# A preactivation convolution stack on one Trainium2 core: casts of tap pieces in GpSimd's row, W loads held during image loads, and another order of the opening

## The chip, the cores and the metric

The kernel runs on one core of one Trainium2 chip. The time is the device time of one execution in microseconds; the figure for a kernel is the median of its runs, and one further execution is recorded by the profiler. The engines are named as the profile names them: PE (TensorE), DVE (VectorE), ACT (ScalarE), POOL (GpSimd) and SP (SyncE, which here issues DMAs and nothing else).

## The reference

Four images of 32 x 32 pixels with 16 channels go through four residual layers. Layers 0 to 2 are of this form (G has other 3x3 taps for every output pixel; M and W join every pixel with every other):

```python
y = group_norm(x)                                        # 8 groups, eps 1e-5
first = jnp.einsum('ijpq,bpqc->bijc', M2, y)
shifted = conv3x3(y, G)            # for every output pixel ij its own 3x3 taps over the whole image
diff = relu(y[:, :, :, None, None, :] - shifted)         # b p q ij c
second = jnp.einsum('ijpq,bpqijc->bijc', W2, diff)
x = x + first - second
```

In layer 3 the group norm is convolved with the impulse response of a recursive filter, which comes from a division of two DFTs, and `x` is added. All is float32; some operands are split into two float32r pieces, `hi` (a cast) and `lo` (what is left), which are multiplied one beside the other.

## The kernel before

**The work of a layer.** A layer has 128 blocks (`NBLK`). A block is 8 output pixels of 16 channels each, so 128 rows of PSUM, with all 1024 pixels of one image in the free dimension. One call of `iteration` does one block for one image. TensorE multiplies the block's taps with the image in a PSUM pair (`pt`, four buffers); VectorE then takes `min(pt, 0) * W` and sums it in one `scalar_tensor_tensor` (L658). The centre pixel is subtracted from the taps beforehand (`minus_mid`, L475), so `pt` is already `shifted - y`.

Images 0 to 2 go through `direct`: two passes with eight of the taps (`f`, L609) and one with the ninth, in float32r pieces (`g`, also L609). Image 3 goes through `shared`, which forms what two neighbouring columns share once (L625), copies it to SBUF with ScalarE (`both_sb`, L629), does the rest (L637) and adds the two with VectorE (L645). The PSUM buffer that L625 wrote comes free with the copy L629.

**Passes.** The first 12 blocks of a layer run for images 0 and 1 and then once more for images 2 and 3; blocks 12 to 115 run for all four; the last 12 run again for (0, 1) and then (2, 3). These five stretches are called sub-passes here; they have 24, 24, 416, 24 and 24 iterations. So the next layer's images 0 and 1 can be normalised, stored and loaded while images 2 and 3 are still being finished, and the other way round.

**Taps.** Four blocks (`GC`) share one chunk of taps; each time a pass comes to a chunk is a "use" `u`, and `begin[u]` is the iteration at which it starts. `four_taps(u)` loads `f` (512 KB, by SP from F) and subtracts the centre on GpSimd (L475). `other_taps(q, at)` makes the pieces of chunk `q`: SP loads `raw` (288 KB from E); GpSimd subtracts the centre (L475) and adds rows (L508 twice); ScalarE casts `hi` (L512); GpSimd subtracts to get `lo` (L514) and issues eight DMAs (L519) that store both in DRAM, in one of eight buffers `gd`. `piece_loads(u)` has SP load `g` from `gd` (L535; 2 DMAs for images 0 and 1 alone, 12 where image 3 takes part). The tiles: `f` three buffers, `g` two, `raw`, `hi` and `lo` one each.

**W.** A W tile is 1 MB (`load_w`, L573, by SP), covers two blocks and has six buffers. `w_loads` issues tile k 24 iterations ahead of its first use (10 for tile 5 and those before it), or later, when a buffer is free.

**Images.** `make_image` runs when a pair of images has finished a layer: `group_norm`; `store_image` (`center` on VectorE, L321, the kinds of shifts and pieces by ScalarE, GpSimd and VectorE, L353 to L372, then three stores to DRAM `img`, L375 to L377); `load_image`, which issues the loads of `f<-img` and `n<-img` (L413) in turn on SP and GpSimd, and for images 2 and 3 on ScalarE too; and `copy_out` (ScalarE, L332), which the next layer's `first_term` reads.

**The order.** The schedule is written by hand, so each engine runs its instructions in the order in which the program issues them. The generators above hang in two lists: `step()`, at the end of each iteration, advances each of them to its next `yield`, and `until(at)` holds one back to iteration `at`. What a generator issues in one step therefore stands in each engine's row ahead of the next iteration's instructions. `other_taps` has its times in the pair `at`, reckoned from `need[q]`, the iteration by which the `g` loads come. Where a DMA's destination or its semaphore isn't free, the queue that issues it stands. The DMAs of SP and ScalarE take turns in eight semaphores: one more is issued only when the one eight places ahead of it has landed.

**The opening.** `first_images` makes images 0 and 1 of layer 0 from host-arranged copies (`first_f`: eight taps and `nine`) without the way through DRAM, and the `g` of uses 0 and 1 from `first_g` (`g9`, cast by ScalarE at L226, `lo` rows by VectorE at L229). Between its group norm's steps TensorE does 16 matmuls of the coefficients' DFT (`coefs`) for layer 3. `rest()` then makes images 2 and 3 by way of DRAM during the first sub-pass.

Of the kernel before, what the change touches and what calls it, by code (L numbers as in the profile page):

```python
# [36 lines left out]
def conv_stack_kernel(ctx, tc, x, M, W, first_w, first_f, first_g, F, E, h0, coef, cst, dft, idp, idq, out):  # L37
# [10 lines left out]
    ge = ctx.enter_context(tc.tile_pool(name="ge", bufs=1))  # L48
    junkp = ctx.enter_context(tc.tile_pool(name="junk", bufs=1))
# [23 lines left out]
    for t in (*yp, *ye):  # L73
# [31 lines left out]
    now = {"at": 0}  # L105
# [86 lines left out]
    def first_images(nine, g9):  # L192
# [21 lines left out]
        def last_tap(b):  # L214
            v, v8 = nine[:, b], ims_of(b)[1].rearrange("p l m -> p (l m)")
# [7 lines left out]

        def first_taps(u):
            part = g9[:, bass.ts(u, GC * P)]
            nc.scalar.copy(gn0[u], part)  # L226
            for r in (32, 96):
                lo = gn0[u][r : r + 32]
                nc.vector.tensor_tensor(lo, part[r : r + 32], lo.bitcast(F32), ALU.subtract)  # L229
            gt[u] = [gn0[u]]  # L230
# [30 lines left out]
        minus_mid(fours[0][:, 1].rearrange("r (n f) -> r n f", f=C), mid, nc.vector)  # L261
# [4 lines left out]
        for _ in range(2):  # L266
            next(norm)
        dft(0, 1)
# [8 lines left out]
        normalise(0, 0, nc.vector)  # L277
        clear(0, 0)
        normalise(0, 1, nc.scalar)
        clear(0, 1)  # L280
# [3 lines left out]
        last_tap(0)  # L284
        for k in range(2):
            normalise(1, k, nc.vector)
            clear(1, k)
# [54 lines left out]
    def store_image(a, xt, neg, rstd):  # L342
# [27 lines left out]
        for b, v in enumerate(kinds):  # L370
            to = kinds_of(ye[a], a, b)
            nc.gpsimd.tensor_copy(to[96:, :, 1:], v[96:, :, :3])  # L372
            nc.scalar.copy(to[:32, :, :3], v[:32, :, 1:])
        rows = img[a]
# [124 lines left out]
    def other_taps(q, at):  # L499
# [3 lines left out]
        raw = ge.tile([96, 3, 2 * P], F32, tag="raw", name="raw")  # L503
# [5 lines left out]
        yield from until(at[1] + 1)  # L509
# [727 lines left out]
```

## Time and profile before

| | us |
|---|---|
| three runs | 3047.81, 3042.73, 3047.37 (median 3047.37) |
| profiled execution | 3047.96, its span 3046.2, mean granted clock 0.991 |
| opening, to the first block | 0 to 16.35 |
| layer 0: sub-passes end | 80.4, 127.0, 919.9, 965.0, 1026.6 |
| layer 1: sub-passes end | 1072.3, 1118.5, 1904.3, 1949.3, 2012.2 |
| layer 2: sub-passes end | 2057.9, 2104.1, 2889.9, 2934.9, 2984.7 |
| layer 3 | 2984.7 to 3046.2 |

The ends are those of VectorE's last L658 in the sub-pass. The profiled execution lies 0.6 us over the median; sums are made against it. In the steady stretch an iteration of `direct` takes 1.93 us and one of `shared` about 1.69 on TensorE, where TensorE sets the pace; a block of images (2, 3) takes 3.75 us, and there VectorE does (three instructions of 1.22 to 1.23 us, with the small ones between). Rows of the profile name line, engine and operation, destination and source, shape and count, then busy time and mean duration, then the engine's idle time ahead of these instructions and what ended most of it. In lists of waits the three figures are the sum, the number and the mean. In timelines a row starts with its time and duration in us, and what the engine waited for stands in brackets.

### The profile page before, as it was taken

How to read it: one execution, taken by the hardware profiler on the slowest of the kernel's cores; microseconds unless marked ns; L12 is line 12 of the kernel's file. 1: busy time of each engine (PE TensorE's matmuls, PEld its weight loads, DVE VectorE, ACT ScalarE, POOL GpSimd, SP SyncE). 2: the span in 40 equal slices, each digit the busy share in tenths (PEclk: the TensorE clock that was granted, in tenths of full speed). 3: DMA queues.
4: the chain of work that ended last, by engine and by line, in shares of the span. 5: the costliest groups of instructions: out<-in, count | busy, mean ns of one | idle time of the engine just before them, and what ended most of it. 6: DMA issues, size and time to landing. Idle time of an engine off the chain costs nothing.

```text
span 3046.2 us, 53601 instructions
## 1 busy us (share of the span) xinstructions
PE 2982.4 (98%) x20884; PEld 2192.1 (72%) x20884; DVE 2412.9 (79%) x3639; ACT 307.5 (10%) x555; POOL 1070.6 (35%) x1517
## 2 busy tenths in 40 slices
PE   7999999999999899999999999989999999999998
PEld 4765666788887576678888888757567888888874
DVE  5878888888887787788888888769788888888873
ACT  1110110000001011000000100101000000000000
POOL 5435663232332433432323233343333233332300
PEclk8999999999999999999999999999999999999998
DMA  8887676656675898766666676589777776857634
GB/s 233 230 207 185 158 189 167 178 154 169 162 164 146 209 224 200 182 155 168 165 158 173 150 180 150 157 198 235 197 179 178 167 185 163 199 151 180 151 107 80
DMA packets 235589, 531.82 MB, mean 175 GB/s; under 512 B 83672, under 2 KB 93496, under 8 KB 209992
## 3 DMA queue, kind: packets, MB, share of 16 engines
q1 hardware_dynamic: 162832, 472.72, 61.3%
q0 software_dynamic: 66480, 47.05, 6.7%
q10 hardware_dynamic: 6024, 8.63, 1.4%
q8 instruction: 165, 2.70, 0.4%
q14 instruction: 88, 0.72, 0.1%
HBM read 481.67 MB, written 45.92 MB: 173 GB/s over the span
## 4 chain that ended last, share of the span: by engine, by line
PE 84%; DVE 3%; DMA 2%; issue 1%; SPq 0%; ACT 0%; POOL 0%; DVEq 0%; POOLq 0%; ACTq 0%
PE pt L609 65%; PE pt L637 14%; PE pt L625 3%; DVE junk L658 2%; PE pt L952 1%; DVE pt L645 1%; DMA f<-img 1%; DMA t<-hd 1%; PE pt L445 0%; DMA g<-gd 0%; SPq L535 0%; DMA raw<-in_E_dram 0%; SPq L413 0%; DVE st L150 0%; POOL raw L508 0%
## 5 line engine op out<-in xcount | busy, mean ns | idle before, releaser
L609 PE MATMUL pt<-f,f 64*128 64x512 f32 x9216 | 2239.4, 592 | 10.3 <-DVE junk L658 4.0
L658 DVE SCALAR_TENSOR_TENSOR junk<-pt,w 128x1024 f32<-128x1024 f32 x1536 | 1880.8, 1224 | 372.7 <-PE pt L609 256.1
L609 PEld LDWEIGHTS pt<-f,f 64*128 64x128 f32 x9216 | 1149.1, 187 | 503.6 <-issue 264.6
L609 PE MATMUL pt<-n,g 64*128 64x480 f32 x2304 | 997.0, 779 | 6.3 <-DMA g<-gd 6.2
L645 DVE TENSOR_TENSOR pt<-pt,both_sb 128x1024 f32<-128x1024 f32 x384 | 473.1, 1232 | 195.2 <-PE pt L637 164.4
L637 PE MATMUL pt<-f,f 64*128 64x256 f32 x3072 | 509.8, 378 | 3.5 <-DVE junk L658 1.2
L637 PE MATMUL pt<-n,g 64*128 64x256 f32 x3072 | 503.4, 372 | 0.0
L629 ACT COPY both_sb<-pt 128x512 f32<-128x512 f32 x384 | 224.9, 586 | 2350.5 <-PE pt L625 2265.3
L609 PEld LDWEIGHTS pt<-n,g 64*128 64x128 f32 x2304 | 314.9, 188 | 188.5 <-issue 102.9
L475 POOL TENSOR_TENSOR raw<-raw,cs 96x256 f32<-96x256 f32 x96 | 69.8, 727 | 908.6 <-DMA raw<-in_E_dram 908.3
L637 PEld LDWEIGHTS pt<-n,g 64*128 64x128 f32 x3072 | 370.2, 188 | 6.3
L514 POOL TENSOR_TENSOR lo<-raw,hi 96x512 fp32r<-96x512 f32 x96 | 121.9, 1270 | 529.3 <-ACT hi L512 529.3
L637 PEld LDWEIGHTS pt<-f,f 64*128 64x128 f32 x3072 | 293.6, 186 | 4.8 <-PE pt L625 2.6
L625 PEld LDWEIGHTS pt<-n,g 64*128 64x128 f32 x2304 | 230.8, 186 | 83.1 <-issue 35.9
L625 PE MATMUL pt<-n,g 64*128 64x256 f32 x2304 | 230.3, 279 | 20.2 <-ACT both_sb L629 20.2
L519 POOL DMA_DIRECT2D gd<-lo x384 | 226.8, 597 | 12.8 <-DMA f<-img 8.1
L519 POOL DMA_DIRECT2D gd<-hi x384 | 229.6, 603 | 3.2 <-issue 3.2
L475 POOL TENSOR_TENSOR f<-f,cs 128x512 f32<-128x512 f32 x113 | 145.6, 1289 | 192.3 <-DMA f<-in_F_dram 167.5
L508 POOL TENSOR_TENSOR raw<-raw 96x256 f32<-96x256 f32 x192 | 139.5, 727 | 15.1
L658 DVE DVE_READ_ACCUMULATOR junk<-pt,w 128x1 f32 x1536 | 127.8, 83 | 0.0
L512 ACT CAST hi<-raw 96x512 fp32r<-96x512 f32 x96 | 59.3, 618 | 189.2 <-POOL raw L508 189.0
L461 POOL DMA_DIRECT2D fd<-ft x48 | 25.2, 533 | 44.2 <-ACT ft L453 27.2
(131 smaller groups left out, 341.2 us busy)
## 6 DMA issues: line engine op xcount, KB each, us to landing
w<-in_W_dram SPq DMA_DIRECT2D x188, 1024.0 KB, 12.1
g<-gd SPq DMA_DIRECT2D x1184, 128.0 KB, 4.3
f<-in_F_dram SPq DMA_DIRECT2D x114, 512.0 KB, 3.6
raw<-in_E_dram SPq DMA_DIRECT2D x96, 288.0 KB, 9.3
gd<-hi POOLq DMA_DIRECT2D x384, 48.0 KB, 4.2
gd<-lo POOLq DMA_DIRECT2D x384, 48.0 KB, 4.5
mt<-in_M_dram SPq DMA_DIRECT2D x12, 512.0 KB, 12.7
w<-in_M_dram SPq DMA_DIRECT2D x12, 512.0 KB, 8.0
```

The costliest lines, as they stand in the source:

```text
L475: engine.tensor_tensor(v, v, m.unsqueeze(1).to_broadcast([v.shape[0], v.shape[1], C]), ALU.subtract)
L508: nc.gpsimd.tensor_tensor(raw[:, 0], raw[:, 0], raw[:, k], ALU.add)
L512: nc.scalar.copy(hi, both)
L514: nc.gpsimd.tensor_tensor(lo, both, hi.bitcast(F32), ALU.subtract)
L519: nc.gpsimd.dma_start(out=to[slot, :, k, :, bass.ts(u, 2 * P)], in_=t[48 * u : 48 * u + 48, slot].bitcast(F32),)
L609: nc.tensor.matmul(pt[:, half, px], lhsT=w[rows, at], rhs=rhs, start=k == 0, stop=k == 2)
L625: nc.tensor.matmul(both[:, half], lhsT=w[rows, at], rhs=ni[rows, dy : dy + 4, 2], start=dy == 0, stop=dy == 2)
L629: nc.scalar.copy(sb, both)
L637: nc.tensor.matmul(pt[:, half].rearrange("p (r k m) -> p k r m", k=2, m=16)[:, k], lhsT=w[rows, at], rhs=rhs, start=k == j == 0, stop=k == ...
L645: nc.vector.tensor_tensor(v, v, sb.rearrange("p h (r m) -> p (h r) m", m=16).unsqueeze(2).to_broadcast([P, 32, 2, 16]), ALU.add,)
L658: nc.vector.scalar_tensor_tensor(junk, pt.rearrange("p h m -> p (h m)"), 0.0, wts[blk // 2][:, blk % 2, :], ALU.min, ALU.mult, accum_out=a ...
L952: nc.tensor.matmul(rows.rearrange("n (j r) -> n j r", j=C)[:, :, 8 * cc :], lhsT=y(cc).rearrange("p q b -> p (q b)"), rhs=ts[k][q][:, :, : ...
```

## The change

- **The cast of the tap pieces.** `hi` is made by GpSimd instead of ScalarE (`nc.gpsimd.tensor_copy`), and `lo` is written in place over `raw`, whose pool has two buffers now. The cast, `lo` and the eight stores follow the additions in the same step; before, they came one and two iterations later. The times `at` are worked out anew: the load of `raw` 34 iterations ahead of the need at most, the rest 15 ahead.
- **W.** `now["image"]` counts images that are being stored and loaded (from `store_image` to the end of `load_image`); `w_loads` issues nothing while it isn't zero.
- **Image loads.** `load_image` issues one image per step, with a `yield` behind each; `copy_out` comes ahead of the loads in `make_image`.
- **The opening.** `g9` and `nine` take tiles of the pool `work` instead of their own; `g9`'s first part is ScalarE's first DMA but x; F of use 0 is loaded ahead of the images, the second part of `coefs` behind image 0 instead of ahead of F, F of use 1 behind image 1 instead of at iteration 2. `minus_mid` of use 0 goes from VectorE to GpSimd. The `lo` rows of `first_taps` become calls of their own (`first_lo`), one of them after `last_tap(0)`. In `rest()` images 0 and 1 are centred and copied out ahead of the store of 2 and 3. `minus_mid` of use 1 comes at iteration 3.
- **Names.** The pair of first images is called `FIRST` (0, 1, as before); the constant 24 of layer 3 is called `AHEAD`; `yq` of layer 3 lies in `ys`.

```diff
+FIRST = (0, 1)
...
+    er = ctx.enter_context(tc.tile_pool(name="er", bufs=2))
...
-    passes = [
-        (blks, batches)
-        for layer in range(3)
-        for blks, batches in (
-            (range(layer * NBLK, layer * NBLK + END), (0, 1)),
-            (range(layer * NBLK, layer * NBLK + END), (2, 3)),
-            (range(layer * NBLK + END, (layer + 1) * NBLK - END), (0, 1, 2, 3)),
-            (range((layer + 1) * NBLK - END, (layer + 1) * NBLK), (0, 1)),
-            (range((layer + 1) * NBLK - END, (layer + 1) * NBLK), (2, 3)),
-        )
-    ]
+    spans = (0, END), (END, NBLK - END), (NBLK - END, NBLK)
+    start = [[range(layer * NBLK + lo, layer * NBLK + hi) for lo, hi in spans] for layer in range(3)]
+    passes = []
+    for layer in range(3):
+        firsts = [FIRST, tuple(b for b in range(B) if b not in FIRST)] if layer == 0 else [(0, 1), (2, 3)]
+        blks = start[layer]
+        passes += [(blks[0], pair) for pair in firsts] + [(blks[1], (0, 1, 2, 3))]
+        passes += [(blks[2], pair) for pair in ((0, 1), (2, 3))]
...
-    now = {"at": 0}
+    now = {"at": 0, "image": 0}
...
+        def first_lo(u, r):
+            part = g9[u]
+            lo = gn0[u][r : r + 32]
+            nc.vector.tensor_tensor(lo, part[r : r + 32], lo.bitcast(F32), ALU.subtract)
+
         def first_taps(u):
-            part = g9[:, bass.ts(u, GC * P)]
-            nc.scalar.copy(gn0[u], part)
-            for r in (32, 96):
-                lo = gn0[u][r : r + 32]
-                nc.vector.tensor_tensor(lo, part[r : r + 32], lo.bitcast(F32), ALU.subtract)
+            nc.scalar.copy(gn0[u], g9[u])
...
-        minus_mid(fours[0][:, 1].rearrange("r (n f) -> r n f", f=C), mid, nc.vector)
+        minus_mid(fours[0][:, 1].rearrange("r (n f) -> r n f", f=C), mid)
...
         first_taps(0)
         for _ in range(2):
             next(norm)
+        first_lo(0, 32)
         dft(0, 1)
...
         last_tap(0)
+        first_lo(0, 96)
...
             first_taps(1)
+            first_lo(1, 32)
+            first_lo(1, 96)
             yield
-            pair = lambda a: (xs[:, 2 * a : 2 * a + 2], *(t[:, 2 * a : 2 * a + 2] for t in (neg, rstd)))
-            yield from store_image(1, *pair(1))
-            yield
-            load_image(0, 1)
-            copy_out(1)
-            yield
-            center(0, *pair(0))
-            yield
-            copy_out(0)
+            for a in range(2):
+                pair = slice(2 * a, 2 * a + 2)
+                at = xs[:, pair], neg[:, pair], rstd[:, pair]
+                later = [b for b in range(2) if 2 * a + b not in FIRST]
+                if later:
+                    yield from store_image(a, *at)
+                    yield
+                    yield from load_image(0, a, later)
+                else:
+                    center(a, *at)
+                    yield
+                copy_out(a)
             nc.vector.tensor_copy(avg_r, avg)
 
         todo.append(rest())
...
         yield from store_image(a, xt, neg, rstd)
+        copy_out(a)
         yield
-        load_image(layer + 1, a)
-        copy_out(a)
...
+        now["image"] += 1
...
-    def load_image(layer, a):
-
-        moves = []
+    def load_image(layer, a, batches=(0, 1)):
+
         of = lambda t: t.rearrange("p l k m -> p l (k m)")
-        for b in range(2):
+        for b in batches:
+            moves = []
...
-        queues = (nc.sync, nc.gpsimd, nc.scalar)[: 2 + a]
-        for n, (to, src) in enumerate(moves):
-            queues[n % len(queues)].dma_start(out=to, in_=src)
+            queues = (nc.sync, nc.gpsimd, nc.scalar)[: 2 + a]
+            for n, (to, src) in enumerate(moves):
+                queues[n % len(queues)].dma_start(out=to, in_=src)
+            yield
+        now["image"] -= 1
...
-        if u == 1:
-            at = 2
-        yield from until(at)
-        load_f(u)
-        yield from until(min(max(at + 8, begin[u] - 16), begin[u] - 2))
+        if u > 1:
+            yield from until(at)
+            load_f(u)
+        yield from until(min(max(at + 8, begin[u] - 16), begin[u] - 2) if u > 1 else 3)
...
-        raw = ge.tile([96, 3, 2 * P], F32, tag="raw", name="raw")
+        raw = er.tile([96, 3, 2 * P], F32, tag="raw", name="raw")
...
         for k in (1, 2):
             nc.gpsimd.tensor_tensor(raw[:, 0], raw[:, 0], raw[:, k], ALU.add)
-        yield from until(at[1] + 1)
         both = raw[:, 0::2]
-        hi, lo = (ge.tile([96, 2, 2 * P], F32R, tag=tag, name=tag) for tag in ("hi", "lo"))
-        nc.scalar.copy(hi, both)
-        yield from until(at[1] + 2)
+        hi, lo = ge.tile([96, 2, 2 * P], F32R, tag="hi", name="hi"), both.bitcast(F32R)
+        nc.gpsimd.tensor_copy(hi, both)
         nc.gpsimd.tensor_tensor(lo, both, hi.bitcast(F32), ALU.subtract)
         to = gd[q % len(gd)]
...
-    at = 0, 1
+    done = [0, 0]
     for q in sorted(need, key=need.get):
+        first = max(need[q] - 34, done[-2])
+        at = first, max(first + 3, need[q] - 15, done[-1])
+        done.append(at[1] + 1)
         tasks.append((at[0], other_taps(q, at)))
-        following = [k for k in sorted(need, key=need.get) if need[k] > need[q]][:1]
-        for k in following:
-            first = max(need[k] - 26, at[1] + 3)
-            at = first, max(first + 4, min(first + 7, need[k] - 9))
...
-            while not w_free():
+            while not w_free() or now["image"]:
...
+        g9 = [work.tile([P, GC * P], F32, tag=tag, name="g9") for tag in ("ft", "xr")]
+        nc.scalar.dma_start(out=g9[0], in_=first_g[:, : GC * P])
...
-        image_tiles(0, 0)
-        image_tiles(0, 1)
-        nine = st.tile([P, 2, 4 * PX], F32, name="nine")
-        g9 = st.tile([P, 2 * GC * P], F32, name="g9")
+        for b in FIRST:
+            image_tiles(0, b)
+        nine = [work.tile([P, 4 * PX], F32, tag=tag, name="nine") for tag in ("yt", "xo")]
         first_part = 4 * P + 2 * NCH
         coefs = st.tile([P, coef.shape[1]], F32, name="coefs")
-        for part in (slice(0, first_part), slice(first_part, coef.shape[1])):
-            nc.sync.dma_start(out=coefs[:, part], in_=coef[:, part])
+        nc.sync.dma_start(out=coefs[:, :first_part], in_=coef[:, :first_part])
+        load_f(0)
         ab = coefs[:, : 2 * P]
         ones = coefs[:, 4 * P : first_part].rearrange("p (ch r) -> p ch r", r=2)
...
-        load_f(0)
         load_first(0)
+        nc.sync.dma_start(out=coefs[:, first_part:], in_=coef[:, first_part:])
         list(load_w(2))
         load_first(1)
-        nc.sync.dma_start(out=g9[:, GC * P :], in_=first_g[:, GC * P :])
+        load_f(1)
+        nc.sync.dma_start(out=g9[1], in_=first_g[:, GC * P :])
         first_images(nine, g9)
...
-            yq = work.tile([P, 16 * (31 + S - FIRST)], F32, name="yq")
+            yq = ys[:, : 16 * (31 + S - AHEAD)]
```

More of the change, by code (lines that the diff above doesn't have):

```diff
@@ L212, in clear, with last_tap @@
                 nc.gpsimd.tensor_tensor(edge, edge, mask.to_broadcast([P, S]), ALU.mult)
-        def last_tap(b):
-            v, v8 = nine[:, b], ims_of(b)[1].rearrange("p l m -> p (l m)")
+        def last_tap(k):
+            b = FIRST[k]
+            v, v8 = nine[k], ims_of(b)[1].rearrange("p l m -> p (l m)")
             m = neg[:, B + b : B + b + 1]
@@ L276, in first_images @@
             neg, rstd = end.value
[L277 to L280, printed above, removed]
+        normalise(FIRST[0], 0, nc.vector)
+        clear(FIRST[0], 0)
+        normalise(FIRST[0], 1, nc.scalar)
+        clear(FIRST[0], 1)
         for ch in range(1, SOON):
@@ L284, in first_images @@
         last_tap(0)
+        first_lo(0, 96)
         for k in range(2):
-            normalise(1, k, nc.vector)
-            clear(1, k)
+            normalise(FIRST[1], k, nc.vector)
+            clear(FIRST[1], k)
         last_tap(1)
@@ L313, in make_image @@
         yield from store_image(a, xt, neg, rstd)
+        copy_out(a)
         yield
-        load_image(layer + 1, a)
-        copy_out(a)
+        yield from load_image(layer + 1, a)
     def center(a, xt, neg, rstd):
@@ L880, in conv_stack_kernel, with load_first @@
         soon = [st.tile([P, 2, 2, 2 * P], F32, name=f"soon{ch}") for ch in range(SOON)]
-        nc.scalar.dma_start(out=g9[:, : GC * P], in_=first_g[:, : GC * P])
-        def load_first(b):
+        def load_first(k):
             size = 8 * PX
-            for to, at in ((ims[0, b][0].rearrange("p l k m -> p (l k m)"), 0), (nine[:, b], 8 * PX)):
-                nc.sync.dma_start(out=to, in_=first_f[:, b, at : at + size])
+            to = ims[0, FIRST[k]][0].rearrange("p l k m -> p (l k m)"), nine[k]
+            for to, at in zip(to, (0, 8 * PX)):
+                nc.sync.dma_start(out=to, in_=first_f[:, k, at : at + size])
                 size = 4 * PX
-        load_f(0)
         load_first(0)
+        nc.sync.dma_start(out=coefs[:, first_part:], in_=coef[:, first_part:])
         list(load_w(2))
         load_first(1)
-        nc.sync.dma_start(out=g9[:, GC * P :], in_=first_g[:, GC * P :])
+        load_f(1)
+        nc.sync.dma_start(out=g9[1], in_=first_g[:, GC * P :])
         first_images(nine, g9)
@@ L908, in conv_stack_kernel @@
     after = (7, 6, 5, 4, 3)
-    FIRST = 24
+    AHEAD = 24
     late, ts = {}, {}
@@ L931, in of_pair @@
         return [
-            (("pair", a), 2 * i + half, y(31 - TQ * k - q - i + 16 * half - FIRST), k, q + i)
+            (("pair", a), 2 * i + half, y(31 - TQ * k - q - i + 16 * half - AHEAD), k, q + i)
             for i in range(2)
@@ L999, in norm3 @@
         for y in (
-            late["yp"][:, a, :, 31 - FIRST :],
+            late["yp"][:, a, :, 31 - AHEAD :],
             late["y3"][:, :, 31:, 2 * a : 2 * a + 2],
@@ L1162 @@
     around = np.zeros((2, S + 2, S + 2, C), x.dtype)
-    around[:, 1 : S + 1, 1 : S + 1] = x[:2]
+    around[:, 1 : S + 1, 1 : S + 1] = x[list(FIRST)]
     taps = lambda tap, half: (
```

## The prediction

> **What bounds the kernel now.** I read the page first, then TensorE's waits, a table by stage, the chain of waits through the worst stage, and last the timeline of the opening.
>
> ```profile
> PE 2982.4 (98%) x20884; PEld 2192.1 (72%) x20884; DVE 2412.9 (79%) x3639; ACT 307.5 (10%) x555; POOL 1070.6 (35%) x1517
> ...
> PEclk8999999999999999999999999999999999999998
> ```
>
> TensorE is the bound, and the change takes no matmul away. What can be won lies in TensorE's waits, in the clock that is halved around them, and in stretches where VectorE is the slower one. TensorE's longest waits:
>
> ```profile
> PE pt L625 <- ACT both_sb L629: 20.2, 2, 10.3
> PE pt L952 <- DMA t<-hd: 8.6, 2, 5.3
> PE pt L609 <- DMA g<-gd: 6.2, 1, 6.2
> ```
>
> Two waits of 10 us lead, on a ScalarE that is 10% busy. They lie in the last sub-pass (images 2 and 3) of layers 0 and 1. The table by stage sets these beside the same sub-pass of layer 2:
>
> ```profile
> 965.00:1026.60 61.60, 49.03 (x396) 36.26 (x394) 47.20 (x81) 10.62 (x23) 29.32 (x46) 0.92 0.88 213
> 1949.30:2012.20 62.90, 49.96 (x399) 36.59 (x396) 47.23 (x82) 10.61 (x23) 29.32 (x46) 0.89 0.89 213
> 2934.90:2984.70 49.80, 46.16 (x414) 34.00 (x411) 47.13 (x81) 7.12 (x13) 1.27 (x1) 1.00 0.38 100
> ```
>
> After the span come busy times of PE, PEld, DVE, ACT, POOL, then clock and DMA. VectorE does 47.1 to 47.2 us in each, so the sub-pass is VectorE's at about 50 us; the first two hold 12 and 13 us more. The chain says why:
>
> ```profile
> 993.38 12.96 DMA f<-img
> ...
> 1009.54 3.48 DMA raw<-in_E_dram
> ...
> 1013.09 0.73 POOL raw L475
> ...
> 1015.96 0.58 ACT both_sb L629
> ```
>
> And ScalarE's timeline, the row ahead of that copy:
>
> ```profile
> 1015.44 0.62 ACT L512 CAST hi<-raw 96x512 fp32r<-96x512 f32 x1 [15.27 <-POOL raw L508]
> ```
>
> SP stands in image loads that share the rings with 1 MB of W (issued 991.90). `raw` is therefore issued at 1009.54, GpSimd's three passes over it (L475, L508 twice, 0.73 us each) end at 1015.4, and the cast of it stands in ScalarE's row ahead of the copy L629 that TensorE needs. Nobody needs the cast so early; the row order alone makes it everyone's wait.
>
> **Part 1, the cast moves from ScalarE to GpSimd, with two raw buffers.** ScalarE loses 96 casts of 618 ns, GpSimd gains 96; `lo` is now written into `raw`. A GpSimd cast of 96x512 is in no row. Below it is the copy 32x480 (584 ns), above it `lo` with two inputs (1270 ns):
>
> ```profile
> L514 POOL TENSOR_TENSOR lo<-raw,hi 96x512 fp32r<-96x512 f32 x96 | 121.9, 1270 | 529.3 <-ACT hi L512 529.3
> ...
> L372 POOL COPY ye<-ys 32x480 f32<-32x480 f32 x7 | 4.0, 584 | 7.6 <-DVE ys L368 7.4
> ```
>
> I take 0.6 us, the nearer in kind. 96 x 0.6 = 58 us on an engine that is 35% busy costs nothing in the middle, where taps lead their use by some 15 iterations (29 us). The gain: in block pair (125, 2/3) VectorE's ends stand 14.72 us apart instead of the 3.75 of its neighbours, 10.97 lost; in layer 1 it is 15.09, and 0.89 at the next, 12.2 lost. A third cast delays `both_sb` at 132.75 (TensorE gap 1.49). Sum: 24.7. It goes if nothing else is late there. Next in line: the taps `g` of block 128. In the new order SP issues two W loads after the image, then F, then this `g`. I put its issue at 1003 to 1005; the W load at 974.50 landed 7.7 us after issue, nearly alone; two of them, F and `g` give 1015 to 1017.5. TensorE, 11 us earlier than now, wants it at 1018.4. It just fits.
>
> The Trainium skill speaks against this move: "GPSIMD Engine Reference", section "Key points", says that GpSimd shares its SBUF interfaces with VectorE and contends with VectorE instructions that have two SBUF inputs, and that elementwise work runs about twice as fast on VectorE. The trace agrees for two SBUF inputs: the two subtracts of L229 took 0.68 and 0.69 us with GpSimd quiet, and 1.33 us for the one at 26.89, beside `lo` on GpSimd. But VectorE's main instruction L658 reads PSUM and SBUF: 1223 ns for the 206 that lie mostly beside GpSimd's adds, 1225 for the 1177 beside none. By the rule a cast would hold VectorE for 0.6 us; some 12 casts fall into VectorE-bound sub-passes, 7 us, and the gain would be 17. By the rows it is nothing; I take the rows.
>
> **Part 2, W waits while an image is in DRAM; each image is loaded in two steps, copied out before.** The 12.96 us that `f<-img` took beside W should fall towards the 3 to 5 us of loads without it. That is off TensorE's path once the cast is gone. The price is W late: W tile 1 of the next layer moves from 991.90 to about 1002, landing near 1010 to 1012, for block 130 at about 1026. Queued behind SP's image loads are those W's, F and `g` above. Covered, by 3 us for `g` and over 10 for W; without the cover each us of lateness is a us lost, and more with the clock.
>
> **Part 3, the opening.** Now TensorE starts blocks at 16.35, and sub-pass 0 of 24 iterations at 1.933 ends at 80.4. Rows that carry it:
>
> ```profile
> 7.50 0.69 DVE L475 TENSOR_TENSOR f<-f,cs 128x512 f32<-128x512 f32 x1 [2.63 <-DMA f<-in_F_dram]
> ...
> 10.61 1.39 DVE L229 TENSOR_TENSOR g<-g,g 32x512 fp32r<-32x512 f32 x2 [1.79 <-ACT g L226]
> ...
> 35.74 1.26 POOL L475 TENSOR_TENSOR f<-f,cs 128x512 f32<-128x512 f32 x1
> ```
>
> The L475 wait leaves VectorE for GpSimd (2 us off the norm), and L229 is split and later. Then the 16 DFT matmuls (0.215 us each, from 20 in 4.30) bind: their coefficients are now loaded after F, f and nine, by bytes near 10.1, so blocks start near 13.6. Iteration 1 ends near 18.0 instead of 22.2: 4 us won, one from the clock. Next, `f` of use 1 leaves its place behind the image store: the gap of 2.42 us at 34.63 goes, and with it a half clock from 37.4 to 40.8, 1.7 us. "TensorE: Matmul & The Clock Gate", section "Why this matters for your kernels", warns of idle gaps over about 3 us; here 2.42 us already had the half clock behind it (0.50 in that stretch). By the rule this edit is worth 2.4, by the trace 4.1. I take the trace.
>
> At nothing I enter `FIRST` (the passes come out the same), `yq` in `ys` (last read by layer 1's store), and images 0 and 1's `center` and `copy_out` ahead of the image store: two L321 in 0.60 us and one L332 at 0.41 in VectorE's and ScalarE's rows, which wait for TensorE there; without that slack, 1 us on the store.
>
> So iteration 16 is reached near 45 instead of 53.5. It needs `f` and `g` of use 2, and here the new order has a price. GpSimd: `raw` for chunk 2 lands near 24.5; add-up, cast, lo 4.4 us; eight stores at 0.6, to 33.9; the same again for chunk 0, to 43.0; image store 3.1; then `f`, ready at 47.5. SP: the fourth `raw` reuses the buffer of chunk 0, which now holds `lo`, so it waits until those stores have landed, near 44.8; behind it in SP's row stand W tile 4, the image stores, F and `g`. `g` also waits for a free DMA semaphore, that of W tile 4: issued 45.3, plus 7.7. `g` issues near 53, behind image stores and F in the rings, and lands near 58.5, against 61.5 now. Then the image loads, 12 us as at 1043 to 1055, W tile 5 near 67, held by the image, landing 75 to 77, and the last six `g` of use 3 behind its semaphore, near 82 to 84, where the first shared block would want them at 78 to 80. Its VectorE end is 85.4 now, 84.5 to 88.5 then. So the 8 us won early are taken back by two `g` waits: I enter a loss of 1 us, from -8 (a gain) to +4.
>
> **Sum.** The profiled execution took 3047.96 (span 3046.2), 0.6 over the median 3047.37 of the runs. 3047.96 - 24.7 + 1 = 3024.3; I say 3024.
>
> **Rivals.** *The opening keeps its gain*: if W tile 4 and the stores land some us sooner, `g` is there near TensorE and 5 to 12 us remain: about 3015. For it: TensorE really is 8 us earlier; against: the queue above. *Transitions half won*: `g` of block 128 comes 3 to 6 us late behind two W's, with the clock 4 to 7 each time: 3024 + 11 = 3035. For it: W's median is 12.1 us to landing, not 7.7. This is also the case in which the change does not do what it says: the stall changes its name. *Slower*: the held W's are the mechanism. If two W's after the image take 14 us each in series (slow tenth of the W loads with a recorded landing), `g` of block 128 lands at 1003 + 28 + 4 = 1035 against 1018: 17 us and 2 of clock in each of two transitions, 38 - 24 = 14 slower, 3061. It decides from 12 us of stall per transition on. Against it: the rings are read in order and few others load then.
>
> **How the numbers follow.** Likeliest case 0.50 (own range 3018 to 3030), kept opening 0.25, half won 0.18, slower 0.03, transitions that lose nearly all they win 0.04 (no change). Range: 3011 to 3036, which leaves out the tails of the second and third case and the last two. Within 0.2% (6 us, about what this measurement can tell from no change): 0.04; faster 0.93, slower 0.03.
>
> **What would show it.** In the trace after: no L629 wait over 2 us; the two sub-passes at 50 to 52 us; no cast on ScalarE; a GpSimd cast of 0.5 to 0.8 us; blocks starting near 13.6; no gap near iteration 8; a `g` wait at iteration 16 of 8 to 12 us, and a short one at the first shared block. Wrong if: `g` of block 128 stops TensorE near 1017; the cast takes over 1 us; sub-pass 0 ends before 75.

## The result, and the profile after

The changed kernel takes 3048.95 us (median of 20 runs, 3043.66 to 3051.64), the kernel before 3045.56 (20 runs, 3040.87 to 3049.29). The ratio is 1.001, with a 95% interval of 1.0003 to 1.0017: slower by about a tenth of a per cent, less than the 0.2% that the prediction set as "no change". Forecast were 3024 and a chance of 0.93 for faster. The profiled execution took 3049.85 us (span 3047.7), 1.9 more than that of before.

The page's first row and clock row hardly differ from before:

```profile
PE 2982.8 (98%) x20884; PEld 2222.2 (73%) x20884; DVE 2413.2 (79%) x3638; ACT 256.4 (8%) x459; POOL 1128.7 (37%) x1617
...
PEclk8999999999999999999999999999999999999999
```

TensorE's waits in the changed kernel (sum, number, longest; the third figure of such a row is the longest single wait, also in the rows further up, where it was called the mean):

```profile
PE pt L616 <- DMA g<-gd: 17.3, 2, 10.6
PE pt L616 <- DVE junk L665: 11.4, 6, 7.4
PE pt L960 <- DMA t<-hd: 8.3, 2, 6.2
PE pt L616 <- DMA gd<-hi: 7.4, 1, 7.4
```

(L616 is the former L609, L665 the former L658, L636 the former L629.) The 20.2 us for `both_sb` are gone, as forecast. In their place stand waits for `g` and for VectorE. (In the fourth row, at 1023.21, the matmul that waits is the one that reads `g`; the releaser named is a store of pieces of another chunk, and the experiments below show which DMA it was.) The table by stage places them; first the transition from layer 0 to layer 1:

```profile
974.20:1024.80 50.60, 46.36 (x390) 34.95 (x387) 47.09 (x81) 9.61 (x21) 29.42 (x47) 1.00 0.87 214
1024.80:1079.80 55.00, 49.19 (x246) 38.53 (x246) 33.04 (x68) 2.77 (x9) 21.99 (x35) 0.91 0.85 202
```

Columns as before: stretch, span, PE, PEld, DVE, ACT, POOL, clock, DMA share, GB/s. The sub-pass (2, 3) lost its 11 us and runs at VectorE's pace; the sub-pass after it, which took 45.7 us before, takes 55.0, at a clock of 0.91. The same ledger for all kernels of this study, from the ends of VectorE's last L665 in each sub-pass of the profiled execution (us):

| kernel | layer 0: sub-pass 0 ends | sub-pass 1 | 2 | 4 | layer 1: 0 | 4 | layer 2: 0 | layer 3 |
|---|---|---|---|---|---|---|---|---|
| before | 80.4 | 46.6 | 792.9 | 61.6 | 45.7 | 62.9 | 45.7 | 61.5 |
| changed | 89.6 | 48.1 | 791.5 | 50.6 | 55.1 | 50.7 | 54.9 | 58.5 |
| 1 before, cast alone | 78.2 | 48.6 | 791.4 | 50.6 | 54.0 | 51.1 | 52.9 | 58.8 |
| 2 before, g first alone | 78.9 | 48.3 | 792.2 | 62.0 | 45.7 | 62.0 | 45.7 | 57.5 |
| 3 before, both | 81.0 | 46.6 | 791.3 | 50.6 | 49.8 | 51.0 | 50.6 | 60.4 |
| 4 changed, cast on ScalarE | 82.8 | 51.1 | 797.3 | 56.9 | 45.7 | 57.8 | 45.7 | 61.2 |
| 5 changed, no hold | 87.5 | 50.0 | 791.5 | 50.6 | 55.5 | 50.7 | 52.6 | 60.7 |
| 6 changed, g first | 84.1 | 51.3 | 791.5 | 50.6 | 50.1 | 50.7 | 49.4 | 58.3 |
| 7 changed, g first, no hold | 87.1 | 50.5 | 791.5 | 50.6 | 47.7 | 50.7 | 48.8 | 59.3 |
| 8 changed, tap times | 67.6 | 52.8 | 791.5 | 50.6 | 55.3 | 50.7 | 55.3 | 58.6 |
| 9 ... and W tile 5 early | 63.5 | 55.6 | 791.5 | 50.6 | 54.6 | 50.7 | 55.3 | 60.8 |
| 10 ... and g first, no hold | 64.7 | 54.7 | 791.5 | 50.6 | 50.4 | 50.7 | 47.3 | 61.3 |
| 11 ... and f ahead of taps | 63.0 | 50.4 | 791.5 | 50.6 | 47.8 | 50.7 | 51.1 | 59.2 |

Sub-pass 3 (45.0), those not listed of layers 1 and 2 and the last (49.8) are the same everywhere within 0.3 us. Layer 3 differs by up to 4 us between kernels with the same instructions there (57.5 to 61.5 in row "before" and rows 1 to 3), so its 3.0 us cannot be called a gain of the change. From before to changed: opening +9.2 and +1.5, sub-pass 2 -1.4, transition 1 -11.0 and +9.4, transition 2 -12.2 and +9.2, layer 3 -3.0: together +1.7, the span's +1.5 within rounding.

Each row of the ledger is a single execution, from 6.6 us under the median of its kernel's runs (row 1) to 4.5 over it (row 5), so the times of whole kernels are compared by the medians. The opening scatters too: SP issues the same loads in the same order in rows "changed", 5, 6 and 7, and sub-pass 0 ends at 84.1 to 89.6. The first two sub-passes together scatter less: they end at 135.4 to 137.7 in these four, and at 126.8 to 127.6 in row "before" and rows 1 to 3.

In the opening the rows of the changed kernel start early, as forecast, and then stop. TensorE's timeline, and SP's:

```profile
10.31 3.79 PE L714 MATMUL pt<-coefs 64*128 64x256 f32 x16 [1.60 <-DMA coefs<-in_coef_dram]
13.88 2.48 PE L616 MATMUL pt<-f,f 64*128 64x512 f32 x8
```

```profile
37.59 9.67 SPq L514 DMA_DIRECT2D raw<-in_E_dram  x2
47.31 0.65 SPq L580 DMA_DIRECT2D w<-in_W_dram  x1
48.08 0.51 SPq L384 DMA_DIRECT2D img<-ys  x1
...
50.22 1.81 SPq L494 DMA_DIRECT2D f<-in_F_dram  x1
58.33 1.76 SPq L543 DMA_DIRECT2D g<-gd  x2
```

Blocks start at 13.88 instead of 16.35, and TensorE begins iteration 16 at 45.4 instead of 53.5. But SP's third and fourth loads of `raw` were issued at 37.59 and 46.94: each stands until the eight stores of the pieces in its buffer have landed, together for 31.1 us and one of them for 22.2:

```profile
SPq L514 <- DMA gd<-raw: 31.1, 2, 22.2
```

All else of SP's row stands behind: W tile 4, the image stores, F, and `g`. `g` also has to wait until W tile 4, eight places ahead of it, has landed (58.25), and TensorE gets it at 61.6. Four iterations on, VectorE stands for W tile 5:

```profile
84.33 1.23 DVE L665 SCALAR_TENSOR_TENSOR junk<-pt,w 128x1024 f32<-128x1024 f32 x1 [12.55 <-DMA w<-in_W_dram]
```

### The profile page after: what moved, and what is told of

It reads as the page before. It is cut to its first block, busy times and chain, and to the rows that moved or that the text cites. A ratio compares the mean times of both kernels' runs of the same rounds, so it can differ in the third digit from the quotient of the medians.

```text
span 3047.7 us, 53387 instructions
## 1 busy us (share of the span) xinstructions
PE 2982.8 (98%) x20884; PEld 2222.2 (73%) x20884; DVE 2413.2 (79%) x3638; ACT 256.4 (8%) x459; POOL 1128.7 (37%) x1617
## 4 chain that ended last, share of the span: by engine, by line
PE 85%; DVE 3%; DMA 2%; POOL 1%; issue 1%; ACT 0%; DVEq 0%; ACTq 0%; SPq 0%; POOLq 0%
PE pt L616 66%; PE pt L644 14%; PE pt L632 3%; DVE junk L665 1%; PE pt L960 1%; DVE pt L652 1%; DMA t<-hd 1%; DMA g<-gd 1%; DMA gd<-hi 1%; PE pt L456 0%; POOL n L422 0%; DMA img<-ys 0%; POOL raw L518 0%; POOL f L422 0%; POOL raw L522 0%
## 5 line engine op out<-in xcount | busy, mean ns | idle before, releaser
L616 PE MATMUL pt<-f,f 64*128 64x512 f32 x9216 | 2245.2, 592 | 14.0 <-DVE junk L665 11.4
L665 DVE SCALAR_TENSOR_TENSOR junk<-pt,w 128x1024 f32<-128x1024 f32 x1536 | 1880.8, 1224 | 403.4 <-PE pt L616 269.8
L616 PEld LDWEIGHTS pt<-f,f 64*128 64x128 f32 x9216 | 1170.1, 187 | 487.2 <-issue 236.5
L616 PE MATMUL pt<-n,g 64*128 64x480 f32 x2304 | 1004.8, 779 | 24.7 <-DMA g<-gd 17.3
L616 PEld LDWEIGHTS pt<-n,g 64*128 64x128 f32 x2304 | 322.3, 188 | 203.3 <-issue 98.6
L636 ACT COPY both_sb<-pt 128x512 f32<-128x512 f32 x384 | 225.2, 586 | 2572.8 <-PE pt L632 2445.5
L644 PEld LDWEIGHTS pt<-n,g 64*128 64x128 f32 x3072 | 371.2, 187 | 4.7
L644 PEld LDWEIGHTS pt<-f,f 64*128 64x128 f32 x3072 | 294.2, 185 | 4.8 <-PE pt L632 2.6
L632 PEld LDWEIGHTS pt<-n,g 64*128 64x128 f32 x2304 | 232.1, 185 | 63.1 <-issue 34.8
L527 POOL DMA_DIRECT2D gd<-raw x384 | 226.7, 597 | 4.2 <-DMA gd<-raw 2.7
L665 DVE DVE_READ_ACCUMULATOR junk<-pt,w 128x1 f32 x1536 | 128.0, 83 | 0.0
L522 POOL TENSOR_TENSOR raw<-raw,hi 96x512 fp32r<-96x512 f32 x96 | 121.7, 1268 | 7.7
L521 POOL CAST hi<-raw 96x512 fp32r<-96x512 f32 x96 | 58.3, 607 | 6.5 <-DMA gd<-hi 0.4
L472 POOL DMA_DIRECT2D fd<-ft x48 | 25.2, 532 | 76.2 <-ACT ft L464 57.8
```

Source lines behind the costliest of these rows:

```text
L521: nc.gpsimd.tensor_copy(hi, both)
L522: nc.gpsimd.tensor_tensor(lo, both, hi.bitcast(F32), ALU.subtract)
L527: nc.gpsimd.dma_start(out=to[slot, :, k, :, bass.ts(u, 2 * P)], in_=t[48 * u : 48 * u + 48, slot].bitcast(F32),)
L616: nc.tensor.matmul(pt[:, half, px], lhsT=w[rows, at], rhs=rhs, start=k == 0, stop=k == 2)
L632: nc.tensor.matmul(both[:, half], lhsT=w[rows, at], rhs=ni[rows, dy : dy + 4, 2], start=dy == 0, stop=dy == 2)
L636: nc.scalar.copy(sb, both)
```

## The experiments

Two questions are open: where the 23 us went that the cast's two waits had cost, and what costs some 10 us in the opening. Theory Q for the first: two waits stood one behind the other in each transition, and the second, for `g` of block 128, was there before the change too, in the shadow of the first. Theory H, against it: the changed kernel's hold on W alone makes the wait for `g`. Each ratio is to the kernel before, timed beside that experiment.

### The transitions

**1. The kernel before with the cast alone moved.**

```diff
-        nc.scalar.copy(hi, both)
+        nc.gpsimd.tensor_copy(hi, both)
```

> The kernel before with one edit: the cast L512 stands in GpSimd's row. Theory Q (the queue): the transition of a layer is bound by the landing of g of block 128, which stands in SP's row behind the image loads, one W tile and F; with the cast gone TensorE merely reaches that g sooner. g lands about 8.9 + 3.7 + 0.8 us (the landings in the changed kernel: first W, F, g) after the W issue at 1010.2, so near 1023.5, and TensorE wants it near 1014: sub-pass 4 of layers 0 and 1 about 50.6 instead of 61.6 and 62.9, the sub-pass behind it 55 to 57 instead of 45.7, and the total 3045 +- 3 (ratio 0.999 to 1.001). Theory H (only the held W's of the changed kernel are guilty): g is there in time with a single W ahead of it, the sub-pass behind stays at 45.7 to 47, total 3022.

Measured: 3042.9 us, ratio 0.9988 (0.998 to 0.9996). Its table by stage, transition 1:

```profile
963.20:1013.80 50.60, 46.45 (x391) 35.13 (x388) 47.07 (x83) 9.59 (x21) 23.18 (x38) 1.00 0.86 211
1013.80:1067.80 54.00, 49.87 (x246) 39.92 (x246) 33.61 (x70) 2.85 (x9) 27.73 (x44) 0.94 0.84 210
```

The single line takes the whole 11.0 us out of the first stretch, and 8.3 of them come back in the next, where TensorE stands for 5.64 us ahead of the ninth tap of block 128 and runs at half clock for 6.8 us after:

```profile
1017.93 1.46 PE L609 MATMUL pt<-n,g 64*128 64x480 f32 x2 [5.64 <-issue]
```

The profile names no releaser for this stop; that it is the landing of `g` is shown by experiments 3 and 6, which move `g` forward. No W is held in this kernel. So the wait is not made by the hold, and theory H falls. The profiled execution (3036.31) was the fastest of 15, so its row in the ledger shows more gain than most runs had; by the medians it is 0.12%, some 4 us.

**2. The kernel before with g ahead of W, cast left on ScalarE.** W isn't issued in iterations 497 to 503, so that F and `g` of block 128 come ahead of the W tile in SP's row; only these rows change place.

```diff
-            while not w_free():
+            while not w_free() or any(497 <= now["at"] - 512 * n < 504 for n in range(2)):
```

> The kernel before with W held from iteration 497 to 504 of layers 0 and 1 alone: F and g of block 128 stand ahead of one W tile in SP's row, and nothing else changes place. The cast stays on ScalarE. By theory Q two waits lie one behind the other in each transition, the cast (10 us) and then g; while the cast holds TensorE to 1016, g lands in its shadow anyway, so taking g's wait away alone wins nothing: sub-pass 4 of layers 0 and 1 at 60 to 63, the next at 45.7 to 46.5, total 3046 +- 3. Rival: raw, which stands ahead of W there, or the image gain from the W that goes later, sub-pass 4 shrinks by 3 us and more, total 3036 to 3041.

Measured: 3045.34 us, ratio 1.0002 (0.9994 to 1.001).

```profile
964.20:1026.20 62.00, 49.95 (x398) 36.70 (x396) 47.25 (x82) 10.63 (x23) 29.33 (x46) 0.92 0.89 219
1026.20:1071.90 45.70, 45.52 (x240) 24.32 (x238) 32.94 (x69) 3.48 (x10) 19.66 (x32) 1.00 0.74 184
```

Taking the second wait away alone wins nothing, since the first covers it.

**3. The kernel before with both edits.**

> The kernel before with both edits: the cast in GpSimd's row and g ahead of W. Cast alone gave 3042.9 (sub-pass 4 at 50.6 and 51.1, the sub-pass behind it at 54.0 and 52.9 instead of 45.7). Theory Q: with g ahead of W the waits of 5.6 and 5.9 us before block 128 shrink to 0 to 2.5 us (g issued near 1011.5, landing near 1015.5, wanted near 1012 to 1014): the sub-pass behind at 46 to 49, total 3042.9 - 12 = 3031 (3027 to 3035), close to the 24.7 us that the prediction entered for the cast less the rest of g's wait. If the two edits do not add up (total over 3038), something else binds the transition.

Measured: 3032.09 us, ratio 0.9963 (0.995 to 0.9977).

```profile
964.00:1014.60 50.60, 46.66 (x391) 35.18 (x388) 47.09 (x81) 9.61 (x21) 23.34 (x39) 1.00 0.85 213
1014.60:1064.30 49.70, 48.22 (x246) 38.01 (x245) 34.59 (x68) 2.86 (x9) 25.30 (x41) 0.97 0.88 220
```

The ratios of the two single edits lie at -0.12% and +0.02%, together they bring -0.37%: two waits in a row, of which only removing both pays. TensorE still stops for `g`, 1.28 and 1.48 us in transition 1, 2.08 and 0.97 in transition 2, which makes 4 to 5 us each with the clock, somewhat more than expected.

**4. The changed kernel with the cast back on ScalarE.**

```diff
-        nc.gpsimd.tensor_copy(hi, both)
+        nc.scalar.copy(hi, both)
```

> The changed kernel with the cast back in ScalarE's row (at the new place in the program, two raw buffers kept). If the engine of the cast is what removed the two 10 us waits: waits of TensorE for L636 (both_sb) come back, 4 us and more in sub-pass 4 of layers 0 and 1 (the additions end at 1001 and 1016, and the cast stands ahead of copies wanted near 997 and 1009), so 55 to 62 instead of 50.6; by theory Q the sub-pass behind gives the same back (46 to 51), and the total stays within 4 us of the changed kernel, 3045 to 3053. If the earlier load of raw is what removed them, sub-pass 4 stays within 2 us of 50.6. If neither hides behind g, the total is 3060 or more.

Measured: 3052.21 us, ratio 1.0015 (1.0008 to 1.0021). TensorE's waits in transition 1:

```profile
PE pt L644 <- ACT both_sb L636: 5.1, 2, 4.9
```

The sub-pass (2, 3) takes 56.9 and 57.8 us, and the next 45.7 with no wait for `g`: the shadow again. The waits are half as long as before (4.87 and 4.95 us against 9.90 and 10.26). So the other edits, the earlier load of `raw` perhaps among them, take away half of each wait; the engine of the cast alone takes away all of it (experiment 1). Sub-pass 2 takes 5.8 us more as well, with a stop of 3.6 us for such a copy at 365.4 and half a clock behind it.

**5. The changed kernel without the hold on W.**

```diff
-            while not w_free() or now["image"]:
+            while not w_free():
```

> The changed kernel without the hold on W (the loop waits for a free buffer only). Its SP row differs from the changed kernel's at the two transitions alone: one W tile ahead of the image loads, one behind, instead of two behind. Theory Q: g still stands behind a W and F, so 0 to 6 us are won over both transitions: sub-pass 0 of layers 1 and 2 at 51 to 55 instead of 55.1 and 54.9; total 3043 to 3049. Theory H: the waits of 7.4 and 6.7 us for g go: 46 to 47 each, total 3030. Both expect nothing in the opening, since SP's row is the same there: sub-pass 0 of layer 0 ends at 89 to 90.

Measured: 3045.54 us, ratio 0.9995 (0.9987 to 1.0003). Transition 1 is as in the changed kernel (55.5), transition 2 is 2.3 us better. That profiled execution (3050.01) lies 4.5 us over its median. By the medians the hold costs about 0.15% (1.001 with it, 0.9995 without; the two intervals touch at 1.0003): some 5 us, not the 18.6 that the two sub-passes lose. SP's row in the opening is the same with and without it, so the hold has no part in the opening's loss.

**6. The changed kernel with g ahead of both W's**, and W held as in the changed kernel besides.

```diff
-            while not w_free() or now["image"]:
+            while not w_free() or now["image"] or any(494 <= now["at"] - 512 * n < 504 for n in range(2)):
```

> The changed kernel with W's loads held on from iteration 494 to 504 of layers 0 and 1 as well, so that F and g of block 128 stand ahead of both W tiles in SP's row (two rows changed place in each transition, nothing else). Theory Q: g is issued near 1012 and lands near 1016 to 1017, behind F alone, and TensorE wants it at 1023: no wait over 1 us; sub-pass 0 of layers 1 and 2 at 46 to 47 instead of 55.1 and 54.9, W tile 66 (needed at iteration 520, some 15 us later) lands in time; total 3048.9 - 18 = 3031 (3028 to 3034). Rival: g is late for another reason (its pieces are stored late, or its own buffer comes free late): the waits stay at 5 us and more, total 3042 to 3049. Second rival: the W tiles become the wait instead: VectorE waits at iteration 516 to 520, 5 us or more each.

Measured: 3037.66 us, ratio 0.9976 (0.9966 to 0.9986). SP's timeline:

```profile
1009.12 0.53 SPq L494 DMA_DIRECT2D f<-in_F_dram  x1
1009.82 1.20 SPq L543 DMA_DIRECT2D g<-gd  x2
1011.12 4.52 SPq L580 DMA_DIRECT2D w<-in_W_dram  x4
1018.95 0.36 SPq L494 DMA_DIRECT2D f<-in_F_dram  x1
1019.52 1.21 SPq L543 DMA_DIRECT2D g<-gd  x2
```

`g` of block 128 was issued at 1009.82 and landed at 1016.3, in 6 us; in the changed kernel it was issued at 1013.07, behind two W's and F, and TensorE got it at 1030.6. So it was late by its place in the row, and not because its pieces were stored late. The rest of the expectation failed: four W tiles now leave in a row, the last of them lands at 1035.92, and the next `g` (issued at 1019.52, landed at 1039.5) is late for block 132, at iteration 520 (the expectation of the next experiment miscounts it as block 136). Of the loss, 4.4 and 3.7 us stay.

**7. g ahead of W, no hold during the image.** One tile goes ahead of the image loads, one less stands behind.

```diff
-            while not w_free() or now["image"]:
+            while not w_free() or any(497 <= now["at"] - 512 * n < 504 for n in range(2)):
```

> The changed kernel with W held from iteration 497 to 504 of layers 0 and 1 alone, and not while an image is in DRAM: in each transition one W tile goes ahead of the image loads, then image, F and g of block 128, then the other W's. Theory Q with a backlog: what is left in the kernel with g first but W held throughout (4.4 and 3.7 us in the next sub-pass, a wait for g of block 136 at iteration 528, behind four W tiles in a row) goes with one tile less behind the image: sub-pass 0 of layers 1 and 2 at 46 to 48 instead of 50.1 and 49.4; sub-pass 4 stays at 50.6; total 3037.7 - 6 = 3032. Rival: the W ahead of the image slows the image's loads (12.96 us for one in the kernel before), and F and g with them: g of block 128 is late again, 51 to 55, total 3040 to 3046.

Measured: 3036.53 us, ratio 0.9969 (0.9959 to 0.9979). The sub-passes after the transitions take 47.7 and 48.8: of 18.6 us lost there, 13.5 are back. The total is 4.5 us over the expectation. Of the 6 us expected beyond experiment 6 the two sub-passes gave 3.0, and the opening, whose order in SP's row is the same, happened to run 3 us longer (87.1).

### The opening

**8. The changed kernel with the tap times of before for chunks 0, 1 and 3.**

```diff
         at = first, max(first + 3, need[q] - 15, done[-1])
+        at = {0: (4, 8), 1: (11, 15), 3: (18, 25)}.get(q, at)
```

> The changed kernel with the times at of chunks 0, 1 and 3 in the opening set to (4, 8), (11, 15) and (18, 25), as the kernel before has them; all else and the rest of the run as changed. In SP's row raw of chunks 1 and 3 no longer stands ahead of W tile 4, the image stores, F and g of use 2, and in GpSimd's row chunk 0 no longer stands ahead of the image store. Theory R (SP stands at raw until the stores of the piece in the same buffer have landed, and GpSimd does chunk 0 first): the image stores are issued near 38.5 instead of 48.1, g of use 2 near 41 instead of 58.3 and lands near 45, where TensorE wants it near 47: the waits of 2.6 (f) and 10.6 us (g) go. W tile 5 then is the next to be late (issued 50 to 56, lands near 62, wanted near 54 to 57): 5 to 8 us. Sub-pass 0 of layer 0 ends at 72 to 78 instead of 82.8 to 89.6 in the kernels with the changed order; total 3049 - 10 = 3039 (3035 to 3043). Rival (the image in DRAM and the rings are the limit, not the standing SP): g comes after 55 all the same, sub-pass 0 ends at 82 or later, total 3045 to 3050.

Measured: 3032.5 us, ratio 0.9959 (0.9946 to 0.9971). SP's timeline, to be held against the changed kernel's above:

```profile
36.90 0.34 SPq L384 DMA_DIRECT2D img<-ys  x1
...
38.93 0.37 SPq L494 DMA_DIRECT2D f<-in_F_dram  x1
39.92 3.96 SPq L543 DMA_DIRECT2D g<-gd  x2
```

The image store goes out 11 us earlier and `g` 18 us earlier; sub-pass 0 ends at 67.6, sooner than the 72 to 78 expected, instead of 89.6 (84.1 to 89.6 in the kernels with that order and the cast on GpSimd), and of that 4.7 are given back in the next. The other edits of the opening are all in, so what cost the changed kernel its opening is the tap times. They act in two places, which this experiment does not separate: the additions of chunk 0 ahead of the image store in GpSimd's row, and loads of `raw` in SP's row that wait for a buffer not yet free. For W tile 5 VectorE now stands 7.5 us and TensorE, which runs ahead of it, 2.3; expected were 5 to 8.

**9. As 8, with W tile 5 issued at iteration 6.**

```diff
-            yield from until(w_first[k] - (24 if k > 5 else 10))
+            yield from until(w_first[k] - (24 if k > 5 else 14 if k > 4 else 10))
```

> As the kernel with the opening's tap times set back, and W tile 5 issued at iteration 6 instead of 10, right behind tile 4 and ahead of the image. If W tile 5 is what is late next: VectorE's wait at block 10 goes, sub-pass 0 of layer 0 ends at 66 to 70, total 3049 - 18 = 3031 with the transitions as in the changed kernel. Rival: the second W in the rings delays the image stores, F and g of use 2 by 6 us (g lands near 51 against 47): 3 to 6 us of it come back at iteration 16, sub-pass 0 ends at 70 to 74.

Measured: 3030.05 us, ratio 0.9952 (0.9938 to 0.9966). Sub-pass 0 ends at 63.5, 4 us sooner (expected: 66 to 70), but TensorE then stands 6.9 us for `f` of use 3, whose subtraction stands in GpSimd's row behind chunk 1's additions and eight stores; sub-pass 1 rises to 55.6. The gain beyond 8 is within what the two medians can tell.

**10. 9 and 7 together.**

> The last two together: opening's tap times, W tile 5 early, g ahead of W in the transitions and no hold during the image. If opening and transitions are independent, the gains add: 3031 - 17 = 3014 (3008 to 3022), over 0.8% under the kernel before. If they share something (the rings are the limit of the whole), it stays above 3025.

Measured: 3018.74 us, ratio 0.9915 (0.9901 to 0.9928). Opening and transitions add up: against the changed kernel's ratio, experiments 9 and 7 bring 0.58% and 0.41%, and both together 0.95%.

**11. As 10, with chunk 1's additions at iteration 17, behind the subtraction for `f` of use 3.**

```diff
-        at = {0: (4, 8), 1: (11, 15), 3: (18, 25)}.get(q, at)
+        at = {0: (4, 8), 1: (11, 17), 3: (18, 25)}.get(q, at)
```

> The kernel with all edits together, and chunk 1's additions at iteration 17 instead of 15, so that GpSimd subtracts the centre of f of use 3 ahead of them (9.1 us of additions, cast, lo and eight stores go behind it). If that place in GpSimd's row is what TensorE waited for at iteration 24 (5.4 us, with 6.8 us of half clock behind it): the wait falls below 1 us, the second sub-pass ends 6 to 8 us sooner (its 54.7 becomes 47 to 49), total 3018.7 - 7 = 3012 (3009 to 3015). Rival: the images 2 and 3 or their g come no sooner (another wait takes its place at iteration 24 to 28): less than 2 us won, 3017 to 3020.

Measured: 3016.24 us, ratio 0.9905 (0.9891 to 0.9918). Sub-pass 1 takes 50.4, 4.3 us less, and the wait for `f` is gone. Both the sub-pass (47 to 49) and the total (3009 to 3015) stay short of the expectation, and the ratio's interval overlaps that of experiment 10, so the gain in the total is not shown. Clock row and the `g` waits that are left:

```profile
PEclk9999999999999999999999999999999999999999
```

```profile
PE pt L617 <- DMA g<-gd: 4.8, 7, 1.1
```

This version has the lowest median of the study, 1% under both kernels.

## Why the prediction was wrong

**The cast: right, to a tenth.** Entered were 10.97, 12.2 and 1.49 us; the three stretches lost 11.0, 12.2 and 1.4. The price of the cast was right too:

```profile
L665 DVE SCALAR_TENSOR_TENSOR junk<-pt,w 128x1024 f32<-128x1024 f32 x1536 | 1880.8, 1224 | 403.4 <-PE pt L616 269.8
...
L521 POOL CAST hi<-raw 96x512 fp32r<-96x512 f32 x96 | 58.3, 607 | 6.5 <-DMA gd<-hi 0.4
```

It takes 0.607 us against the 0.6 taken from the copy, and L665 keeps its 1224 ns; the 35 of them that overlap a cast by over 0.2 us take 1223.3 on average, the others 1224.5. The prediction called this a choice of the rows over the rule. But the Trainium skill ("GPSIMD Engine Reference", section "Key points") names VectorE instructions with two SBUF inputs, or in a 2-port mode, and L665 reads PSUM and SBUF: the 7 us that the prediction drew from the rule did not follow from it, and page and trace agree.

**The failing step of part 2: "It just fits."** The prediction did ask what is late next, named `g` of block 128 and put its issue at 1003 to 1005. In the changed kernel that sub-pass begins 9.2 us later; less this shift, the issue was at 1003.9. The image loads also fell as forecast, `f<-img` on SP from up to 12.96 us to 4.3 to 5.2; without the hold (experiment 5) image loads beside W took up to 9.8. Two terms of the step were wrong.

The first is the due time. TensorE, "11 us earlier than now", was said to want this `g` at 1018.4. But the kernel before takes it at 1025.13, as the matmuls of block 128's first iteration show:

```profile
1023.81 1.89 PE L609 MATMUL pt<-f,f 64*128 64x512 f32 x8
1025.13 0.79 PE L609 MATMUL pt<-n,g 64*128 64x480 f32 x2
```

Less 11 us, that is 1014.1, and 1014.0 was measured (1023.2 less the shift). The due time was put 4.4 us too late; against the right one, the prediction's own landing would have been 1 to 3 us late.

The second is the landing. It was put at 1015 to 1017.5, and was 1021.4 less the shift: a W that landed "nearly alone" in 7.7 us was taken as the measure, while the first W behind the image landed 8.9 us after its issue, the second 6.2 us later and F 3.7 after that (the first issued at 1011.03; landed 1019.91, 1026.08, 1029.76), and `g` last. The landings on record of SP's DMAs in this kernel, 866, all come in the order of issue, so `g` has to wait for all that stands ahead of it. A cover of 1 to 3 us between two estimates became a lateness of 7.4, and half a clock for 10.2 us. Two waits of 7.4 and 6.7 took back 18.6 of 23.2 us.

The rival "half won" (3 to 6 us late, 4 to 7 with the clock) had the mechanism and came short of the size; "slower" had 17 us a transition. The case that the transitions lose nearly all they win, given 4 in 100, is nearly what they did. Experiment 1 adds what no rival said: this wait was already in the kernel before, hidden behind the cast's. The hold, which the prediction charged with it, only adds a second W (some 5 us by experiment 5).

**The failing step of part 3: a landing time with no user.** The waits that the prediction saw go at iterations 0 and 8 went, and its sketch was right up to iteration 16: blocks at 13.88 (13.6), iteration 16 at 45.4 (45), `f` of use 2 at 49.05 (47.5), SP held until 46.9 (44.8), `g` landed at 61.56 (58.5). W tile 4 took 10.9 us and not the 7.7 entered, which carried the rest 3 to 5 us on. Then the sum priced the `g` of use 3 behind W tile 5, and not tile 5 itself, though its landing (75 to 77) stood there: block 10 begins at iteration 20, and VectorE was free for it at 71.8, 10.2 us behind the landing of `g`. In the prediction's own times that is 58.5 + 10.2 = 68.7, an estimate by which tile 5 is already 6 to 8 us late. VectorE started at 84.33, 12.55 us late, and TensorE stood 7.4 of them. Entered for the opening was a loss of 1, at worst 4; it was 9.2 in sub-pass 0 and 1.5 in the next, and 8 to 11 for both together in the four executions with this order. The text also said that the image holds tile 5 back; experiment 5 shows that its place in SP's row is the same without the hold. What delays it is SP's standing for `raw`, which experiment 8 takes away.

**The range.** In both parts each DMA was entered as if it landed with the rings (the queues of the DMA engines) nearly empty, at the moments when most was queued; and in both a due time was wrong or not asked. The two risks were put together as if independent, with 0.04 for no change.

## What to carry to other kernels

When a wait is about to be removed, look for the second one that ends in its shadow: list, for the stretch after it, each transfer with its issue, the megabytes queued ahead of it, and the moment the freed engine wants it. A landing time in the working needs a user and a due time beside it, read from a row of the trace, or it is not priced. In a row that is executed in order, put the load that is needed first at the front (here 128 KB ahead of 1 MB), and issue nothing there that waits for a buffer while something urgent stands behind it.

## What the runs showed of the hardware

Short stops of TensorE cost clock, but not each of them: a stop of 2.29 us at 2988.04 in the changed kernel had 3.4 us at half clock behind it, one of 2.2 us at 47.3 in experiment 10 had none, and two of 1.15 and 1.06 us within 2.7 us in experiment 11 had 3.4. The half-clock stretches came in multiples of 3.4 us (3.4, 6.8, 10.2, 13.7, 17.1).
